# Convolution on one core: the overlap copied out once and added in PSUM to permuted block rows, one GELU per pass, group norm's sums on ScalarE

## Chip, cores and metric

The kernel runs on one core of one Trainium2 chip, as one program. The metric is device time in microseconds, the median of a few runs. TensorE (PE), VectorE (DVE), ScalarE (ACT) and GpSimd (POOL) are the engines; SP issues most of the loads.

## The reference

Two residual layers on `x` of shape 32 x 128 x 32 x 32 (32 images, 128 channels, L = 1,024 positions). Only the first layer matters here, and only up to the GELU:

```
u = group_norm(x)                         # 32 groups of 4 channels, per image
h = einsum('bdl,de->ble', u, W_enc) + b_enc        # 1,024 features
K = table of 64 taps per feature (from dt, A, C)
y = causal convolution of h with K along l, per feature
y = gelu_tanh(y + D * h)
...                                       # GLU, layer norm, decode, residual
...                                       # second layer: group norm, deformable convolution
```

## The kernel before, in words

The program has four parts in order. `ssm_kernel_table` works out the convolution's taps and writes them to `kp_d`. `normalise_input` runs group norm on each of the 32 images and stores the result in `u_d`. `ssm_convolution` reads `u_d` and writes the activated convolution to `y_d`. `main_block` does everything else: gated linear unit, layer norm, decode, and the second layer, in an order that is written out by hand. The first three parts are ordered by a scheduler, which lists the instructions of each engine from its own model of their times; every engine then works through its list in order.

`group_norm` (L161) takes one image of 128 partitions x 1,024. It sums the rows on VectorE (L164), averages over the four channels of a group with a matmul by `gavg` (L166), copies the mean (L168), subtracts it into `gn_cen` (L170), squares and sums on ScalarE (L173), averages again (L174), takes the root (L176) and the reciprocal (L177), and scales (L178). The pool has three buffers for each tile. The main block has a group norm of its own, in steps; `group_norm` is called apart from `normalise_input` only in a fallback branch.

`ssm_convolution` makes eight passes (`k`), each over 128 of the 1,024 features, and in each pass first encodes and then convolves.

- `encode(k)` goes over the 32 images and two halves of the sequence. Four matmuls (L227) fill a PSUM tile `psz` with 4 blocks of 128 positions x 128 features, and VectorE adds the bias and writes the tile into `z` (L234), with the image as the innermost index. After it, `z[0]` and `z[1]` hold for each feature a matrix of 128 positions by (4 blocks x 32 images).
- `convolve(k, z)` goes over 16 groups of `CG` = 8 features, each in two quarters (`q`) of `QC` = 4 features and two halves of the sequence (`i`). One such unit is one PSUM tile `psy` of two banks; three of them exist. Four matmuls (L266), one a feature, each multiply `z` by a Toeplitz table `toe` of 128 x 192: the 192 columns are the 128 outputs of a block and 64 outputs that reach over into the next block. The profile shows each of these matmuls as two records. The partitions of a unit are four blocks of 32 images, in the order of the sequence.

The 64 columns that reach over (`RW` = 64) must be added to the block that follows, which lies 32 partitions further. Before, a tile `t` in SBUF collects them: its first 32 rows are zeros written by GpSimd (`i` = 0, L275) or a copy from the end of the half before, out of that half's PSUM tile `last` (L277, VectorE); its other rows are three copies of 32 rows from PSUM (L280; the first on VectorE, the other two on ScalarE). VectorE then adds the unit's own columns (L284). ScalarE makes the GELU in two pieces, L286 from PSUM and L290 from `t`, and reverses the columns on the way. The result goes to `yo` (two tiles a group, four buffers), and GpSimd issues eight stores a group, one per tile and block (L296).

Of the kernel before, what the change touches and what calls it, by code (L numbers as in the profile page):

```python
# [7 lines left out]
F32 = mybir.dt.float32  # L8
AF = mybir.ActivationFunctionType
ALU = mybir.AluOpType  # L10
AX = mybir.AxisListType
# [3 lines left out]
P = 128  # L15
B, C, H, W = 32, 128, 32, 32
L = H * W
# [8 lines left out]
TW = 192  # L26
# [3 lines left out]
CG = 8  # L30
# [130 lines left out]
def group_norm(nc, pool, psum, gavg, eps, xt, out):  # L161

    s = pool.tile([P, 1], F32, tag="gn_s", name="gn_s")
    nc.vector.reduce_sum(s, xt, axis=AX.X)  # L164
    pm = psum.tile([P, 2], F32, tag="gn_ps", name="gn_ps")
    nc.tensor.matmul(pm[:, 0:1], gavg, s, start=True, stop=True)  # L166
    m = pool.tile([P, 1], F32, tag="gn_m", name="gn_m")
    nc.vector.tensor_copy(m, pm[:, 0:1])  # L168
    cen = pool.tile([P, L], F32, tag="gn_cen", name="gn_cen")
    nc.vector.tensor_scalar(cen, xt, m, None, op0=ALU.subtract)  # L170
    sq = pool.tile([P, L], F32, tag="gn_sq", name="gn_sq")
    ss = pool.tile([P, 1], F32, tag="gn_ss", name="gn_ss")
    nc.scalar.activation(sq, cen, AF.Square, accum_out=ss)  # L173
    nc.tensor.matmul(pm[:, 1:2], gavg, ss, start=True, stop=True)  # L174
    r = pool.tile([P, 1], F32, tag="gn_r", name="gn_r")
    nc.scalar.activation(r, pm[:, 1:2], AF.Sqrt, bias=eps)  # L176
    nc.vector.reciprocal(r, r)  # L177
    nc.vector.tensor_scalar(out, cen, r, None, op0=ALU.mult)  # L178


def normalise_input(nc, tc, const, x, u_d):

    with tc.tile_pool(name="gna", bufs=3) as pool, tc.tile_pool(
        name="gna_ps", bufs=2, space=PSUM
    ) as psum:
        for b in range(B):
            xt = pool.tile([P, L], F32, tag="xt", name=f"xt_{b}")
            nc.sync.dma_start(xt, x[b])
            u = pool.tile([P, L], F32, tag="u", name=f"u_{b}")
            group_norm(nc, pool, psum, const["gavg"], const["eps"], xt, u)  # L190
            nc.scalar.dma_start(u_d[b], u)


def ssm_convolution(nc, tc, ins, u_d, kp_d, y_d):

    NB = NJ // 2  # L200
    RW = TW - P
    QC = 4
    with tc.tile_pool(name="cv1", bufs=1) as one, tc.tile_pool(
        name="cvu", bufs=4
    ) as up, tc.tile_pool(name="cvt", bufs=3) as tp, tc.tile_pool(
        name="cvy", bufs=4
    ) as yp, tc.tile_pool(
        name="cv_psz", bufs=2, space=PSUM
    ) as psz, tc.tile_pool(name="cv_psy", bufs=3, space=PSUM) as psy:
        w_enc = one.tile([P, D], F32, tag="w_enc", name="w_enc")  # L210
        nc.sync.dma_start(w_enc, ins["W_enc"])
        b_enc = one.tile([P, D], F32, tag="b_enc", name="b_enc")
        nc.sync.dma_start(b_enc, ins["b_enc_row"].to_broadcast([P, D]))

        def encode(k):

            z = [
                one.tile([P, P, NB, B], F32, tag=f"z{g}", name=f"z_{k}_{g}") for g in range(2)
            ]
            bias = b_enc[:, k * P : (k + 1) * P]  # L220
            for b in range(B):
                u = up.tile([P, L], F32, tag="u", name=f"u_{k}_{b}")
                nc.sync.dma_start(u, u_d[b])
                for g in range(2):
                    ps = psz.tile([P, NB, P], F32, tag="ps", name=f"psz_{k}_{b}_{g}")
                    for j in range(NB):
                        nc.tensor.matmul(  # L227
                            ps[:, j, :],
                            u[:, (NB * g + j) * P : (NB * g + j + 1) * P],
                            w_enc[:, k * P : (k + 1) * P],  # L230
                            start=True,
                            stop=True,
                        )
                    nc.vector.tensor_add(  # L234
                        z[g][:, :, :, b].rearrange("p d j -> p j d"),
                        ps,
                        bias[:, None, :].to_broadcast([P, NB, P]),
                    )
            return z

        def convolve(k, z):
            rows = [t.rearrange("p d j b -> p d (j b)") for t in z]
            for g in range(P // CG):
                d0 = k * P + g * CG
                toe = tp.tile([P, CG, TW], F32, tag="toe", name=f"toe_{d0}")
                table = kp_d[d0 : d0 + CG, 0:TW]

                nc.sync.dma_start(
                    toe,
                    bass.AP(  # L250
                        tensor=table.tensor,
                        offset=table.offset,
                        ap=[[1, P], [KPW, CG], [1, TW]],
                    ),
                )
                yo = [
                    yp.tile([P, CG, P], F32, tag="yo", name=f"yo_{d0}_{i}") for i in range(2)
                ]
                for q in range(CG // QC):
                    c0 = q * QC  # L260
                    last = None
                    for i in range(2):
                        ps = psy.tile([P, 2, 512], F32, tag="ps", name=f"psy_{d0}_{q}_{i}")
                        ps = ps[:, :, : 2 * TW].rearrange("p h (c n) -> p h c n", c=2)
                        for c in range(QC):
                            nc.tensor.matmul(  # L266
                                ps[:, c // 2, c % 2, :],
                                rows[i][:, g * CG + c0 + c, :],
                                toe[:, c0 + c, :],
                                start=True,  # L270
                                stop=True,
                            )
                        t = tp.tile([P, 2, 2, RW], F32, tag=f"t{i}", name=f"t_{d0}_{q}_{i}")
                        if i == 0:
                            nc.gpsimd.memset(t[0:B], 0.0)  # L275
                        else:
                            nc.vector.tensor_copy(t[0:B], last[P - B : P, :, :, :RW])  # L277
                        for j in range(1, NB):
                            copy = nc.scalar.copy if j > 1 else nc.vector.tensor_copy
                            copy(  # L280
                                t[j * B : (j + 1) * B],
                                ps[(j - 1) * B : j * B, :, :, :RW],
                            )
                        nc.vector.tensor_add(t, t, ps[:, :, :, P:TW])  # L284
                        to = yo[i][:, c0 : c0 + QC, :].rearrange("p (h c) l -> p h c l", c=2)
                        nc.scalar.activation(  # L286
                            to[:, :, :, RW:P], ps[:, :, :, RW:P][:, :, :, ::-1],
                            AF.Gelu_apprx_tanh,
                        )
                        nc.scalar.activation(  # L290
                            to[:, :, :, 0:RW], t[:, :, :, ::-1], AF.Gelu_apprx_tanh
                        )
                        last = ps
                for i in range(2):
                    for j in range(NB):
                        nc.gpsimd.dma_start(  # L296
                            y_d[d0 : d0 + CG, :, i * NB + j, :].rearrange("d b l -> b d l"),
                            yo[i][j * B : (j + 1) * B],
                        )

        for k in range(KD):
            convolve(k, encode(k))


def deformable_general(nc, tc, const, ins, x1_d, out, image):
# [7 lines left out]
    with tc.tile_pool(name="gdf1", bufs=1) as one, tc.tile_pool(  # L313
# [27 lines left out]
        def prepare(b):  # L341

            xt = two.tile([P, L], F32, tag="xt", name=f"gen_dx_{b}")
            nc.sync.dma_start(xt, x1_d[bass.ds(image, 1)].rearrange("o c l -> (o c) l"))
            v = one.tile([P, L], F32, tag="v", name=f"gen_dv_{b}")
            group_norm(nc, one, psum, const["gavg"], const["eps"], xt, v)

            vT = two.tile([P, NCHUNK, C], F32, tag="vT", name=f"gen_dvT_{b}")
# [903 lines left out]
```

## Time and profile before

| | us |
|---|---|
| three runs: median (lowest, highest) | 14067.17 (14044.14, 14073.55) |
| profiled execution | 14059.14 |
| its span | 14057.0 |
| start to the first encode matmul (tables, group norm) | 178 |
| convolution, from there to the first instructions of the main block | 1,614 |
| main block | 12,265 |

Over the whole span TensorE is busy for 94%, VectorE for 63%, ScalarE for 23% and GpSimd for 65%. The shares differ by stage: in the convolution TensorE is busy for 1,370 of 1,614 us, with a granted clock of 0.95.

How to read the lines. A line of a timeline has the start, the busy time, the engine, the source line and operation, the tiles (written <- read), their shape and a count; in brackets the idle time before it and what ended that. A line of the chain of waits has start, length and what the chain went through. A group line has engine, operation, tiles, shapes and count, then the total busy time in us and the mean of one in ns, then the idle time before it in us by what ended it. A line of stages has the window, its length, and the busy time and count of PE, PE weight loads, DVE, ACT and POOL, then the granted TensorE clock, the share of the DMA engines and the rate.

### The profile page before, as it was taken

To read this page: it belongs to the slowest core of one execution; us is meant where nothing else is said; L and a number is where in the kernel's file an instruction comes from. 1 tells how busy PE (TensorE), PEld (TensorE's weight loads), DVE (VectorE), ACT (ScalarE), POOL (GpSimd) and SP (SyncE) were. 2 spreads that over 40 slices of the span, in tenths; PEclk is the share of its full clock that TensorE was granted. 3 is DMA by queue.
4 is the path that set the end of the run, shared out by engine and by line. 5 is a ranking of instruction groups with operands and counts; after the bars stand their busy time and mean duration, and the time that the engine had idled before them with its cause. 6 is when DMAs were issued, how large, how long until landed. Compare 5 with 4: busy or idle time off the path is not lost.

```text
span 14057.0 us, 134776 instructions
## 1 busy us (share of the span) xinstructions
PE 13268.5 (94%) x40482; PEld 7317.0 (52%) x40482; DVE 8827.7 (63%) x12555; ACT 3215.1 (23%) x5422; POOL 9113.7 (65%) x9158
## 2 busy tenths in 40 slices
PE   5888889999999999999999999999999999999965
PEld 4777744555555555555555555555555555555532
DVE  6666614666666666666666666666666666666655
ACT  3445412222222222222222121222222222222210
POOL 1334413777777777777777777777777777777767
PEclk9999999999999999999999999999999999999977
DMA  6777724888888888888888888888888888889888
GB/s 224 232 232 230 222 79 126 239 237 235 233 231 232 231 233 238 236 235 230 231 232 229 229 229 230 229 234 237 239 236 233 230 233 231 233 236 237 233 228 227
DMA packets 1741840, 3172.55 MB, mean 226 GB/s; under 512 B 311218, under 2 KB 1030450, under 8 KB 1740082
## 3 DMA queue, kind: packets, MB, share of 16 engines
q1 hardware_dynamic: 1528498, 2708.63, 72.9%
q10 hardware_dynamic: 163456, 320.92, 6.4%
q0 software_dynamic: 49152, 134.28, 3.1%
q8 instruction: 329, 5.39, 0.2%
q14 instruction: 405, 3.32, 0.1%
HBM read 2697.07 MB, written 466.06 MB: 225 GB/s over the span
## 4 chain that ended last, share of the span: by engine, by line
PE 75%; DMA 10%; DVE 7%; POOL 3%; issue 2%; ACT 2%; SPq 1%; DVEq 0%; ACTq 0%; POOLq 0%
PE gpg L707 22%; PE gpv L730 21%; PE dps L1032 21%; DMA ds<-dhat 6%; PE psz L227 4%; PE gph L746 3%; PE gpo L639 3%; DVE dco L839 2%; DVE ds L989 2%; POOL y_d L296 1%; DMA y_d<-yo 1%; PE psy L266 1%; DVE dp L1035 1%; ACT t L280 1%; DMA dhy<-dhat 1%
## 5 line engine op out<-in xcount | busy, mean ns | idle before, releaser
L1032 PE MATMUL dps<-ds,dxw 128*128 128x256 f32 (+18 forms) x13056 | 4737.7, 450 | 308.0 <-DVE dp L1035 305.7
L1035 DVE TENSOR_TENSOR dp<-dps,k_weight_slots 128x256 f32<-128x256 f32 (+17 forms) x6528 | 3061.5, 485 | 2868.8 <-PE dps L1032 2578.2
L1049 POOL TENSOR_TENSOR dacc<-dacc,dp 128x256 f32<-128x256 f32 (+3 forms) x4736 | 4224.6, 892 | 371.4
L1044 POOL TENSOR_TENSOR dp<-dp 128x512 f32<-128x512 f32 (+3 forms) x2176 | 2858.6, 1314 | 2159.3 <-DVE dp L1035 2140.9
L1032 PEld LDWEIGHTS dps<-ds,dxw 128*128 128x128 f32 x13056 | 2478.6, 193 | 3330.7 <-issue 2510.7
L707 PE MATMUL gpg<-gy,g_w_glu 128*128 128x512 f32 x8192 | 3986.6, 593 | 19.1 <-DMA gy<-y_d 14.3
L730 PE MATMUL gpv<-gy,g_w_glu 128*128 128x512 f32 x8192 | 3975.3, 592 | 0.0
L989 DVE TENSOR_TENSOR ds<-ds,dhy 128x1024 f32<-128x1024 f32 (+3 forms) x2176 | 3158.0, 1451 | 1242.4 <-DMA ds<-dhat 1165.3
L707 PEld LDWEIGHTS gpg<-gy,g_w_glu 128*128 128x128 f32 x8192 | 1544.6, 190 | 1235.2 <-issue 974.2
L730 PEld LDWEIGHTS gpv<-gy,g_w_glu 128*128 128x128 f32 x8192 | 1548.9, 189 | 1158.2 <-issue 915.2
L767 ACT ACTIVATE gq<-gr 128x512 f32<-128x512 f32 x448 | 282.3, 630 | 5050.9 <-DVE gr L759 4725.9
L768 POOL TENSOR_TENSOR gs<-gs,gq 128x512 f32<-128x512 f32 x448 | 599.1, 1337 | 1267.2 <-ACT gq L767 1267.1
L266 PE MATMUL psy<-toe,z 128*128 128x192 f32 x4096 | 790.2, 353 | 222.9 <-DVE t L277 214.8
L266 PEld LDWEIGHTS psy<-toe,z 128*128 128x128 f32 x4096 | 735.5, 207 | 273.4 <-issue 211.1
L714 ACT ACTIVATE gs<-gpg,k_b_glu 128x512 f32<-128x512 f32 x512 | 351.8, 687 | 2151.3 <-PE gpg L707 2078.9
L903 ACT ACTIVATE dh<-dr,k_minus 128x624 f32<-128x624 f32 x768 | 620.5, 808 | 933.4 <-DMA dr<-rel_d 493.5
L296 POOL DMA_DIRECT2D y_d<-yo x1024 | 589.1, 583 | 351.8 <-ACT yo L290 324.2
L738 DVE SCALAR_TENSOR_TENSOR gs<-gpv,k_b_glu,gs 128x512 f32<-128x512 f32 x512 | 379.9, 742 | 413.8 <-PE gpv L730 413.8
L641 POOL TENSOR_TENSOR gs<-gs,gr 128x512 f32<-128x512 f32 x448 | 635.3, 1418 | 0.0
L904 ACT ACTIVATE dh<-dh,one 128x624 f32<-128x624 f32 x768 | 626.3, 815 | 25.0
L227 PE MATMUL psz<-w_enc,u 128*128 128x128 f32 x4096 | 584.5, 288 | 24.0 <-DVE z L234 9.1
L275 POOL MEMSET t<- 32x256 f32 x256 | 72.4, 322 | 776.0 <-ACT yo L290 775.1
(164 smaller groups left out, 6620.3 us busy)
## 6 DMA issues: line engine op xcount, KB each, us to landing
dhy<-dhat SPq DMA_DIRECT2D x1536, 512.0 KB
ds<-dhat SPq DMA_DIRECT2D x1536, 512.0 KB
dhat<-dh ACTq DMA_DIRECT2D x768, 312.0 KB
u<-u_d SPq DMA_DIRECT2D x256, 512.0 KB
y_d<-yo POOLq DMA_DIRECT2D x1024, 128.0 KB, 3.7
gy<-y_d SPq DMA_DIRECT2D x512, 256.0 KB
toe<-kp_d SPq DMA_DIRECT2D x128, 768.0 KB
dxw<-dvt_d SPq DMA_DIRECT2D x1248, 64.0 KB
```

The lines of the kernel that those rows point to most:

```text
L227: nc.tensor.matmul(ps[:, j, :], u[:, (NB * g + j) * P : (NB * g + j + 1) * P], w_enc[:, k * P : (k + 1) * P], start=True, stop=True,)
L266: nc.tensor.matmul(ps[:, c // 2, c % 2, :], rows[i][:, g * CG + c0 + c, :], toe[:, c0 + c, :], start=True, stop=True,)
L296: nc.gpsimd.dma_start(y_d[d0 : d0 + CG, :, i * NB + j, :].rearrange("d b l -> b d l"), yo[i][j * B : (j + 1) * B],)
L641: nc.gpsimd.tensor_add(sums[0], sums[0], r)
L707: nc.tensor.matmul(gate, w_glu[:, k, D + m * P : D + m * P + P], ys[k], start=(k == 0), stop=(k == KD - 1),)
L730: nc.tensor.matmul(val, w_glu[:, k, m * P : m * P + P], ys[k], start=(k == 0), stop=(k == KD - 1),)
L904: nc.scalar.activation(t, t, AF.Relu, scale=-1.0, bias=const["one"])
L989: nc.vector.tensor_mul(s[:, :m], s[:, :m], hy[:, :m])
L1032: nc.tensor.matmul(ps, xw[:, j, :], s[:, :m, :, y0 : y0 + ny], start=True, stop=True)
L1035: nc.vector.tensor_mul(prod[:, :m, :, y0 : y0 + ny], ps, w[:, :, :, None].to_broadcast([P, m, KY2, ny]),)
L1044: nc.gpsimd.tensor_add(prod[:, :m, 0], prod[:, :m, 0], prod[:, :m, 1])
L1049: nc.gpsimd.tensor_add(to, to, prod[:, slot : slot + nj, 0])
```

## The change

In `group_norm`, both sums move to ScalarE: an Identity pass over the image with an accumulator, and a Square pass with the negated mean as bias, both writing into the output tile as scratch. The negated mean is made by ScalarE; the subtracted copy `gn_cen` and `gn_sq` are gone, and the last instruction adds the negated mean and scales in one.

In the convolution, the blocks of a half are laid on the partitions in the order 0, 2, 1, 3, by permuting the encode's columns and the stores' targets. The 64 columns that reach over are copied out of PSUM in one ScalarE copy of all 128 partitions. VectorE then adds them in place into the unit's own columns in PSUM: in this order blocks 0 and 2 (partitions 0 to 63) go to blocks 1 and 3 (partitions 64 to 127) in one add, block 1 goes to block 2 in a second, and the end of the half before goes to block 0 in a third (for `i` = 1 only). One GELU of 128 columns a feature follows. The memset and `last`'s hold on the PSUM tile are gone.

```diff
 def group_norm(nc, pool, psum, gavg, eps, xt, out):
     s = pool.tile([P, 1], F32, tag="gn_s", name="gn_s")
-    nc.vector.reduce_sum(s, xt, axis=AX.X)
+    nc.scalar.activation(out, xt, AF.Identity, accum_out=s)
...
-    nc.vector.tensor_copy(m, pm[:, 0:1])
-    cen = pool.tile([P, L], F32, tag="gn_cen", name="gn_cen")
-    nc.vector.tensor_scalar(cen, xt, m, None, op0=ALU.subtract)
-    sq = pool.tile([P, L], F32, tag="gn_sq", name="gn_sq")
+    nm = pool.tile([P, 1], F32, tag="gn_m", name="gn_m")
+    nc.scalar.mul(nm, pm[:, 0:1], -1.0)
     ss = pool.tile([P, 1], F32, tag="gn_ss", name="gn_ss")
-    nc.scalar.activation(sq, cen, AF.Square, accum_out=ss)
+    nc.scalar.activation(out, xt, AF.Square, bias=nm, accum_out=ss)
...
-    nc.vector.tensor_scalar(out, cen, r, None, op0=ALU.mult)
+    nc.vector.tensor_scalar(out, xt, nm, r, op0=ALU.add, op1=ALU.mult)
...
+    ORDER = (0, 2, 1, 3)
...
-                            u[:, (NB * g + j) * P : (NB * g + j + 1) * P],
+                            u[:, (NB * g + ORDER[j]) * P : (NB * g + ORDER[j] + 1) * P],
...
-                        t = tp.tile([P, 2, 2, RW], F32, tag=f"t{i}", name=f"t_{d0}_{q}_{i}")
-                        if i == 0:
-                            nc.gpsimd.memset(t[0:B], 0.0)
-                        else:
-                            nc.vector.tensor_copy(t[0:B], last[P - B : P, :, :, :RW])
-                        for j in range(1, NB):
-                            copy = nc.scalar.copy if j > 1 else nc.vector.tensor_copy
-                            copy(
-                                t[j * B : (j + 1) * B],
-                                ps[(j - 1) * B : j * B, :, :, :RW],
-                            )
-                        nc.vector.tensor_add(t, t, ps[:, :, :, P:TW])
-                        to = yo[i][:, c0 : c0 + QC, :].rearrange("p (h c) l -> p h c l", c=2)
+                        over = tp.tile([P, 2, 2, RW], F32, tag=f"t{i}", name=f"t_{d0}_{q}_{i}")
+                        nc.scalar.copy(over, ps[:, :, :, :RW])
+
+                        def carry(to, rows, src):
+                            own = ps[to : to + rows, :, :, P:TW]
+                            nc.vector.tensor_add(own, own, src)
+
+                        carry(64, 64, over[0:64])
+                        carry(32, 32, over[64:96])
+                        if i > 0:
+                            carry(0, 32, last[96:P])
                         nc.scalar.activation(
-                            to[:, :, :, RW:P], ps[:, :, :, RW:P][:, :, :, ::-1],
+                            yo[i][:, c0 : c0 + QC, :].rearrange("p (h c) l -> p h c l", c=2),
+                            ps[:, :, :, RW:TW][:, :, :, ::-1],
                             AF.Gelu_apprx_tanh,
                         )
-                        nc.scalar.activation(
-                            to[:, :, :, 0:RW], t[:, :, :, ::-1], AF.Gelu_apprx_tanh
-                        )
-                        last = ps
+                        last = over
...
-                            y_d[d0 : d0 + CG, :, i * NB + j, :].rearrange("d b l -> b d l"),
+                            y_d[d0 : d0 + CG, :, i * NB + ORDER[j], :].rearrange("d b l -> b d l"),
```

More of the change, by code (lines that the diff above doesn't have):

```diff
@@ L163, in group_norm @@
     s = pool.tile([P, 1], F32, tag="gn_s", name="gn_s")
-    nc.vector.reduce_sum(s, xt, axis=AX.X)
+    nc.scalar.activation(out, xt, AF.Identity, accum_out=s)
     pm = psum.tile([P, 2], F32, tag="gn_ps", name="gn_ps")
     nc.tensor.matmul(pm[:, 0:1], gavg, s, start=True, stop=True)
-    m = pool.tile([P, 1], F32, tag="gn_m", name="gn_m")
-    nc.vector.tensor_copy(m, pm[:, 0:1])
-    cen = pool.tile([P, L], F32, tag="gn_cen", name="gn_cen")
-    nc.vector.tensor_scalar(cen, xt, m, None, op0=ALU.subtract)
-    sq = pool.tile([P, L], F32, tag="gn_sq", name="gn_sq")
+    nm = pool.tile([P, 1], F32, tag="gn_m", name="gn_m")
+    nc.scalar.mul(nm, pm[:, 0:1], -1.0)
     ss = pool.tile([P, 1], F32, tag="gn_ss", name="gn_ss")
-    nc.scalar.activation(sq, cen, AF.Square, accum_out=ss)
+    nc.scalar.activation(out, xt, AF.Square, bias=nm, accum_out=ss)
     nc.tensor.matmul(pm[:, 1:2], gavg, ss, start=True, stop=True)
```

## The prediction

> **What bounds the kernel now.** I read the stages first, then the convolution stage's matmuls, its chain of waits and its operations. The stages (window, then busy microseconds by engine, clock, DMA share, GB/s):
>
> ```profile
> 0.00:178.00 178.00, 34.82 (x129) 31.11 (x129) 119.03 (x216) 56.37 (x109) 3.17 (x8) 1.00 0.65 228
> 178.00:1792.00 1614.00, 1369.70 (x8192) 1234.46 (x8192) 1063.00 (x1793) 710.96 (x2049) 660.41 (x1278) 0.95 0.76 227
> 1792.00:14057.00 12265.00, 11864.00 (x32162) 6051.47 (x32162) 7645.70 (x10546) 2447.76 (x3264) 8450.08 (x7873) 0.99 0.84 225
> ```
>
> The edit reaches 1,792 us of 14,057. The main block behind it has, in the built changed kernel, the same instructions in the same order. A convolution pass takes 201 us (first encode matmul at 177.97, last tile at 1788.5, eight passes): some 74 us encode, some 127 us convolve. A pass convolves 16 groups of 4 units; a unit is one PSUM tile, written by 8 matmul records. The timeline of TensorE in one pass:
>
> ```profile
> 875.17 7.12 PE L266 MATMUL psy<-toe,z 128*128 128x192 f32 x32 [2.85 <-DVE t L277]
> 882.74 5.81 PE L266 MATMUL psy<-toe,z 128*128 128x192 f32 x32 [0.45 <-DVE t L277]
> 891.89 7.12 PE L266 MATMUL psy<-toe,z 128*128 128x192 f32 x32 [3.34 <-DVE t L277]
> ...
> 941.73 5.44 PE L266 MATMUL psy<-toe,z 128*128 128x192 f32 x32 [3.34 <-DVE t L277]
> ```
>
> A line of 32 is one group. It goes in 5.44 us at best: 0.165 us a record, **1.31 us a unit** back to back, about 1.57 us from the start of a lone unit to its data. Every second group TensorE waits some 3.3 us, and then mostly runs its first records slowly (7.12 against 5.44). A pair takes 16.4 to 17.0 us: **8.22 us a group** (mean of the six pairs from 875.17 to 973.88). The chain of waits says why:
>
> ```profile
> 871.08 2.30 POOL y_d L296 x4
> 873.38 0.33 POOL t L275
> 873.71 0.02 issue
> 873.73 0.43 DVE t L284
> 874.16 0.02 issue
> 874.19 0.39 ACT yo L286
> 874.58 0.02 issue
> 874.60 0.44 DVE t L277
> 875.04 0.14 issue
> 875.17 2.87 PE psy L266 x8
> ```
>
> GpSimd zeroes the next pair's tiles only behind 16 stores; add, GELU and the copy of `last` wait for that, and so does the PSUM tile that TensorE needs.
>
> **What the skill says.** (1) "TensorE: Matmul & The Clock Gate", section "What's actually happening": the array drops to half clock after about 3.4 us of idleness and comes back after as long a busy stretch. The trace agrees in kind: pauses of 2.85 to 3.34 us are followed by slow records, though not always (941.73). (2) "PSUM — Partial Sum Buffer", "Engine vs sequencer instructions": ScalarE and VectorE are strict FIFO. In the windows read here their records keep the built order, so a built order may be read as a chain.
>
> **The change, part by part.** Durations of the convolution's operations, in the stage's groups:
>
> ```profile
> L280 ACT COPY t<-psy 32x256 f32<-32x256 f32 x1024 | 370.5, 362 | 696.9 <-DVE t L280 682.4
> L284 DVE TENSOR_TENSOR t<-t,psy 128x256 f32<-128x256 f32 x512 | 210.4, 420 | 268.8 <-ACT t L280 178.3 <-POOL t L275 87.1 <-ACT yo L286 0.7
> L286 ACT ACTIVATE yo<-psy 128x256 f32<-128x256 f32 x512 | 195.2, 381 | 211.6 <-DVE t L284 209.4
> ```
>
> *ScalarE.* Before, a unit has two copies and two GELUs (0.362 x 2 + 0.381 + 0.410 = 1.52 us). After, one copy of 128x256 (taken as 0.362, the partition count being no part of it) and one GELU of 128x512: 0.381 plus 256 elements at 0.833 ns (the skill's "ScalarE: Activation LUTs", "What ACT_TABLE_LOAD costs"; the trace has 1,055 ns for 1,024 and 630 for 512, or 0.830) = **0.594 us**. So 0.96 us a unit, 3.8 of some 8 us a group: this saving is off the path, but its duration is in the loop below.
>
> *VectorE.* Ten instructions a group before (4 L280, 2 L277, 4 L284), ten after: two adds per unit, three for the second half. Same count, no gain by itself. They write PSUM in place, which no record shows. Low end 0.42 (L284). The skill's "Perfetto Trace Analysis", "Optimizing Scalar/DVE Operations", gives 125 ns overhead on PSUM against 60 on SBUF: 0.49. High end 0.60: the encode add (1,045 ns for 512 elements with strided writes) less 0.15 fixed, scaled to 256. I take 0.45 start to start, as two of these instructions in a row take now.
>
> *GpSimd.* 256 memsets leave (72.4 us of its time), and with them the 3.3 us wait. Its stores stay: 8 x 0.583 = 4.66 us a group. A landing takes 3.7 us, and an output buffer is wanted again two groups later, some 12 us after its last GELU: covered up to landings of about 8.
>
> *What is late next.* In the built changed kernel ScalarE's list in 13 of 16 groups reads: GELU 0, GELU 2, copy 3, copy 0', GELU 1, GELU 3, copy 1', copy 2' (a prime is the next group). With three PSUM tiles, GELUs 0 and 2 free two, TensorE fills 3 and 0', and GELU 1, which frees the third, stands behind copy 0'. So half a loop is GELU 0.594 + release 0.06 + one unit issued 1.31 + the next one's data 1.57 + 0.03 + copy 0.362 + 0.02 = 3.95 us. **7.89 us a group**, with TensorE idle for 1.33 us twice. VectorE has room in it: with both copies of a pair 1.31 us apart and adds of d, GELU 2 ends 5d - 0.66 after the second copy, and TensorE is free for 0' at 1.96, so d may be 0.52.
>
> The sum for a pass:
> - 13 groups x (8.22 - 7.89) = -4.3 us.
> - The first three groups stand in another order (each GELU behind the copy two units on), which TensorE sets: 5.3 + 5.3 + 6.5 = 17.1 us. Before, 859.80 to 875.17 plus half of 16.7 = 23.7: -6.6.
> - The built order puts two encode tiles of the next pass ahead of the last unit. Each waits for a VectorE add (1.045 + 0.1) and takes TensorE 1.0 us; part of that is encode work done early: +3.5.
>
> That is -7.4 us a pass, **-59 us** for eight.
>
> *Permuted blocks* (the encode's column order, the stores' targets) keep count, size and shape of every matmul and DMA: nothing, whatever covers them.
>
> *Group norm.* VectorE loses a reduce (1.216), a subtract (0.744) and a copy an image; ScalarE gains an Identity pass and a small multiply. The stage now runs at 7.40 us per two images: the chain has the load of `xt` at 104.66 and again at 112.06, 4.55 us each, after the subtract that frees the buffer. After, `xt` is held to the last scale. In the built order, three images a round: Identity 1.06, store issue 0.34, mean back at 1.71, negate 0.15, Identity 1.06, Square 1.15, negate 0.15, Identity 1.06, Sqrt done at 5.5, VectorE's reciprocal and scale to 6.5, load 4.55: 11.1 us, 3.70 an image, as now. I put +5 us on it for ScalarE's queue, which now also holds the stores behind these passes (bounds -5 and +20). The copy of group norm in the fallback branch does not run: the trace has no record of it.
>
> Together -54 us. The profiled execution took 14,059 us (span 14,057), so 14,005; the median of the runs, 14,067, lies 8 us higher: **14,012 us**.
>
> **The rivals.**
> *Slower: the adds in PSUM are dear.* From d = 0.52 each further 0.01 us costs 0.05 us a group in 13 x 8 groups, 5.2 us, more once GELU 3 waits too. Break-even is near d = 0.61, and 0.66 gives +40 us: 14,110. For it: VectorE's adds stand between ScalarE's two instructions in every unit. Against: reading PSUM costs nothing visible now (0.420). Chance 0.09.
> *Slower: TensorE goes to half clock in its 1.33 us gaps.* One slow first unit a group costs 1.3 to 1.7 us (7.12 against 5.81 and 5.44): +140 us over 104 groups, 14,150. The end of the main block is the nearest case:
>
> ```profile
> 13604.91 3.57 PE L1032 MATMUL dps<-ds,dxw 128*128 128x288 f32 x6 [4.33 <-DVE dp L1035]
> 13609.67 3.57 PE L1032 MATMUL dps<-ds,dxw 128*128 128x352 f32 x6 [1.20 <-DVE dp L1035]
> 13614.40 1.97 PE L1032 MATMUL dps<-ds,dxw 128*128 128x416 f32 x6 [1.16 <-DVE dp L1035]
> 13618.40 2.34 PE L1032 MATMUL dps<-ds,dxw 128*128 128x480 f32 x6 [2.03 <-DVE dp L1035]
> ```
>
> Once quick, it stays quick over 1.16 and 2.03 us. Chance 0.06.
> *No change:* each of the loop's two halves being 0.2 us longer (GELU of reversed rows, copy) takes back 42 us, or landings slow beyond 8 us and GELUs wait for stores. 14,067, chance 0.17.
> *TensorE-bound throughout*, 5.3 us a group, as its idle time alone would promise: 2.6 x 104 = 270 us more, 13,740. ScalarE's order speaks against it. Chance 0.03.
>
> **How the numbers follow.** My forecast has 0.65, between 13,960 and 14,045 by the spread of the loop's terms (0.15 us in a half is 31 us) and of the first groups (3 us a pass). The range 13,935 to 14,105 takes in the no-change case and part of the dear adds, and leaves out the half clock and the TensorE-bound case. About 0.2%, 28 us, is what a measurement of this kernel can tell from no change. Faster by more: 0.67; within: 0.17; slower: 0.16.
>
> **What would show it.** Right: no wait on a memset; groups of matmuls split in pairs of units with gaps near 1.3 us, ended by GELU; in-place adds at 0.42 to 0.5; passes of some 194 us; the clock at 1.00 there. Wrong: adds above 0.6, slow matmuls after short gaps, idle time ended by stores, or normalisation longer than 150 us.

## The result, and the profile after

The changed kernel takes 14,004.9 us (median of four runs, 13,995.6 to 14,027.6), the kernel before 14,058.7 in four runs: a ratio of 0.9964, 95% interval 0.9947 to 0.9981. That is 54 us less. The forecast was 14,012 us and 55 us below the 14,067 known then.

The profiled execution of the changed kernel is the slowest of its four (14,027.6 us, span 14,025.8), so the two profiles differ by 31 us only. By the starts of TensorE's first records in each stage:

| us | before | after | difference |
|---|---|---|---|
| start to the first encode matmul | 178.0 | 200.7 | +22.8 |
| first encode matmul to the last of the convolution | 1,607.6 | 1,557.3 | -50.4 |
| from there to the main block's first matmul | 36.8 | 39.9 | +3.1 |
| main block | 12,234.6 | 12,227.9 | -6.7 |

The main block has the same instructions in the same order in both. The profiles of all fourteen kernels in this study, which share the main block, give 12,208 to 12,240 us for it, so the last row says nothing. The first two rows are far clearer than the medians.

The stages of the changed kernel (window, busy us by engine PE, weight loads, DVE, ACT, POOL, then clock, DMA share, GB/s):

```profile
0.00:178.00 178.00, 33.26 (x114) 28.48 (x114) 59.09 (x110) 87.93 (x183) 2.43 (x5) 1.00 0.57 202
178.00:1792.00 1614.00, 1305.43 (x8238) 1175.68 (x8238) 1083.93 (x1815) 470.80 (x1049) 590.15 (x1025) 0.98 0.77 236
```

In the first window VectorE's work has halved (119 to 59 us) and ScalarE's has grown (56 to 88), but the window moves fewer bytes: group norm has become slower. In the second the clock has risen from 0.95 to 0.98 and GpSimd has lost the 70 us of its zeros. (While passes are convolved the clock is 1.00, in 862:984 for instance; what is missing lies at the ends of passes, see below.)

TensorE's timeline in the pass that the prediction showed:

```profile
886.47 2.87 PE L266 MATMUL psy<-toe,z 128*128 128x192 f32 x16 [1.02 <-ACT yo L284]
890.36 2.87 PE L266 MATMUL psy<-toe,z 128*128 128x192 f32 x16 [1.02 <-ACT yo L284]
...
979.90 1.16 PE L227 MATMUL psz<-w_enc,u 128*128 128x128 f32 x8 [1.22 <-DVE z L234]
982.34 1.16 PE L227 MATMUL psz<-w_enc,u 128*128 128x128 f32 x8 [1.28 <-DVE z L234]
983.34 1.47 PE L266 MATMUL psy<-toe,z 128*128 128x192 f32 x8
```

The groups of 32 with a pause of 3.3 us in every second one are gone. There are pairs of units (16 records, 2.87 us) and 1.02 us of waiting for a GELU after each: 3.885 us from pair to pair (half of the loop of one group), **7.77 us a group**. No pair is slow. The last three lines are the end of the pass: two encode tiles ahead of the last unit, each after a wait for VectorE's add. The chain of waits of one half of the loop:

```profile
909.12 0.61 ACT yo L284
...
909.78 2.88 PE psy L266 x16
...
912.74 0.04 ACT t L274
...
913.01 0.61 ACT yo L284
...
913.66 1.58 PE psy L266 x8
```

A GELU frees a tile, TensorE fills two units, the copy of the second goes through ScalarE, and only behind it stands the next GELU that frees a tile. The convolution's operations (idle time before them behind the second bar):

```profile
L278 DVE TENSOR_TENSOR psy<-psy,t 32x256 f32<-32x256 f32 x768 | 327.3, 426 | 26.2
L284 ACT ACTIVATE yo<-psy 128x512 f32<-128x512 f32 x512 | 296.1, 602 | 103.7 <-DVE psy L278 101.8 <-DMA y_d<-yo 0.5
L278 DVE TENSOR_TENSOR psy<-psy,t 64x256 f32<-64x256 f32 x512 | 226.6, 443 | 364.8 <-ACT t L274 356.3
L274 ACT COPY t<-psy 128x256 f32<-128x256 f32 x512 | 190.5, 372 | 1004.7 <-PE psy L266 1004.7
```

The adds in PSUM cost 0.43 to 0.44 us, the GELU 0.602, the copy 0.372. ScalarE's GELUs wait for VectorE (101.8 us in all), not for stores (0.5); its copies wait for TensorE. The chain of waits in group norm:

```profile
144.47 6.62 DMA u_d<-u
...
151.11 1.15 ACT u L164 x2
152.26 0.15 ACT gn_r L173
152.40 1.12 ACT u L170 x2
153.52 4.72 DMA xt<-in_x
...
158.27 6.17 DMA u_d<-u
```

Here a store and a load alternate. The Identity pass of a round's third image writes into the output tile `u`, so it waits until the store of three images before has landed. The first image's root and scale stand behind it, then comes the load of the image that follows, and behind that image's Identity pass the next store is issued (158.27, though its data was ready at 157.8). A round of three images takes 12.3 to 13.8 us (the last seven rounds, 13.1 in the mean); before, three images took about 11.4 (the last twelve images).

### The profile page after: what moved, and what is told of

It reads as the page before. It is cut to its first block, busy times and chain, and to the rows that moved or that the text cites. A ratio compares the mean times of both kernels' runs of the same rounds, so it can differ in the third digit from the quotient of the medians.

```text
span 14025.8 us, 133165 instructions
## 1 busy us (share of the span) xinstructions
PE 13195.7 (94%) x40482; PEld 7248.1 (52%) x40482; DVE 8797.9 (63%) x12459; ACT 3004.9 (21%) x4494; POOL 9042.0 (64%) x8902
## 4 chain that ended last, share of the span: by engine, by line
PE 76%; DMA 10%; DVE 9%; issue 2%; POOL 1%; ACT 1%; SPq 1%; DVEq 0%; ACTq 0%; POOLq 0%
PE gpg L703 23%; PE gpv L726 21%; PE dps L1028 21%; DMA ds<-dhat 5%; PE gph L742 3%; PE gpo L635 3%; PE psy L266 2%; PE psz L227 2%; DMA y_d<-yo 2%; DVE z L234 2%; DVE dco L835 2%; DVE ds L985 2%; DVE dp L1031 1%; DVE psy L278 1%; DMA dhy<-dhat 1%
## 5 line engine op out<-in xcount | busy, mean ns | idle before, releaser
L266 PE MATMUL psy<-toe,z 128*128 128x192 f32 x4096 | 734.0, 333 | 203.3 <-ACT yo L284 203.1
L266 PEld LDWEIGHTS psy<-toe,z 128*128 128x128 f32 x4096 | 662.8, 191 | 268.8 <-ACT yo L284 266.8
L278 DVE TENSOR_TENSOR psy<-psy,t 32x256 f32<-32x256 f32 (+1 forms) x1280 | 553.9, 433 | 391.0 <-ACT t L274 356.3
```

The costliest lines, as they stand in the source:

```text
L266: nc.tensor.matmul(ps[:, c // 2, c % 2, :], rows[i][:, g * CG + c0 + c, :], toe[:, c0 + c, :], start=True, stop=True,)
L278: nc.vector.tensor_add(own, own, src)
```

## The experiments

Kernels whose convolution is ordered by hand begin to encode at 189 to 194 us instead of 175 with the same group norm, so the time of a pass compares them best. Their group norm, still left to the scheduler, takes 8.3 to 8.7 us for two images where conv_alone takes 7.3 (the last twelve images of each).

| kernel | median us | ratio to before (95%) | first encode | us a group |
|---|---|---|---|---|
| conv_alone | 13,988.9 | 0.9958 (0.9941 to 0.9974) | 174.9 | 7.77 |
| norm_scratch | 14,007.1 | 0.9963 (0.9949 to 0.9977) | 191.3 | 7.77 |
| norm_bufs | 13,980.6 | 0.9941 (0.9924 to 0.9957) | 161.3 | 7.77 |
| hand_built | 14,043.4 | 0.9989 (0.9982 to 0.9996) | 193.2 | 7.77 |
| gelu_split | 14,058.5 | 0.9997 (0.9988 to 1.0006) | 193.4 | 7.89 |
| adds_more | 14,042.9 | 0.9988 (0.9980 to 0.9997) | 175.1 | 8.08 |
| hand_unit | 13,862.0 | 0.9862 (0.9844 to 0.9879) | 189.4 | 6.3 |
| hand_unit_yo6 | 13,797.0 | 0.9812 (0.9796 to 0.9828) | 193.6 | 5.8 |
| memset_dve | 14,363.2 | 1.0211 (1.0193 to 1.0228) | 174.6 | 11.5 |
| hand_before | 14,088.4 | 1.0018 (1.0010 to 1.0025) | 190.4 | 8.1 |
| hand_before_early | 13,995.8 | 0.9961 (0.9946 to 0.9975) | 189.2 | 7.3 |
| best | 13,756.1 | 0.9783 (0.9767 to 0.9799) | 156.8 | 5.8 |

(In hand_unit, hand_unit_yo6, hand_before, hand_before_early and best, us a group is the time of convolving a pass, first matmul of it to the next pass's first encode, over 16.)

**conv_alone: the convolution's part alone.** The edit puts the old `group_norm` back.

```diff
-    nc.scalar.activation(out, xt, AF.Identity, accum_out=s)
+    nc.vector.reduce_sum(s, xt, axis=AX.X)
...
```

> The changed convolution with the group norm of before. In the changed kernel the first encode matmul starts at 200.7 us (before: 178.0) and the convolution takes 1,557 us (before: 1,608). If the two parts are independent, the first encode starts at 178 (176 to 181) and the convolution keeps 1,557 (1,550 to 1,565): some 23 us faster than the changed kernel, about 13,982 against a 14,005 and 0.9945 of before. Rival: the late start is partly given back in the convolution (loads that had more time), then the convolution takes 1,570 to 1,580 here and the gain over the changed kernel is under 10 us.

The first encode starts at 174.9 us, just ahead of the 176 expected, and the convolution takes 1,556.0 us against 1,557.3. The parts are independent: what group norm loses is not given back later. The whole gain is the convolution's, and the median is 16 us below the changed kernel's, where 23 were expected.

**norm_scratch: a scratch tile for the two passes of group norm.**

```diff
+    sq = pool.tile([P, L], F32, tag="gn_sq", name="gn_sq")
-    nc.scalar.activation(out, xt, AF.Identity, accum_out=s)
+    nc.scalar.activation(sq, xt, AF.Identity, accum_out=s)
```

> The changed kernel, with a scratch tile of its own for the outputs of the Identity and the Square pass in group norm, instead of the output tile. Theory: a round of three images takes 13.4 us because the Identity pass of the third image waits for the store of the output tile of three images before (6.2 us from issue to landing), and with it on ScalarE's queue the Sqrt of the first image, its scale and then the load of the next image (5.0 us), behind whose Identity the next store stands: 6.2 + 2.4 + 5.0. Without the hold on the output tile the round falls to about 11.1 us and the first encode starts at 178 (175 to 184); no Identity waits for a store. Rival: ScalarE's longer list and the later release of the input tile set the round by themselves: the first encode stays at 196 to 201.

The first encode starts at 191.3 us, between the two expectations. No Identity pass waits for a store any more, and a round falls from 13.1 to 11.9 us, not to 11.1. So the hold of the store on `u` is 9 of the 23 us. The rest hangs on the load: in the chain of this kernel it takes 6.7 us from an image's Identity pass to its scale and the issue of the load that this releases, and 5.06 for the load.

**norm_bufs: six buffers in group norm's pool instead of three.**

```diff
-    with tc.tile_pool(name="gna", bufs=3) as pool, tc.tile_pool(
+    with tc.tile_pool(name="gna", bufs=6) as pool, tc.tile_pool(
```

> The changed kernel with six instead of three buffers for group norm's tiles. With a scratch tile of its own a round of three images fell from 13.4 to 11.9 us only; what was left went over a load: the Sqrt of the first image stands behind the Identity pass of the third, and the input tile is free only after the scale behind it (7.1 us after the image's start, then 4.8 us of load). Theory: with six buffers neither the load nor the store is waited for, and ScalarE's own work of about 3.2 us an image sets the pace: the first encode starts at 160 to 172 us, before the 178 of before. Rival: the waits between ScalarE and TensorE inside an image (0.68 us each) or the DMA rate hold it at 3.7 us or more an image: 178 or later.

The first encode starts at 161.3 us, 39 us earlier than in the changed kernel and 17 earlier than before. ScalarE's waits in the stage (us in all, times, longest) show why, first in the changed kernel, then here:

```profile
ACT u L164 <- DMA xt<-in_x: 26.3, 20, 5.2
ACT u L164 <- DMA u_d<-u: 10.6, 8, 3.2
```

```profile
ACT u L164 <- DMA xt<-in_x: 1.1, 2, 0.7
```

No row for stores is left. ScalarE now works through two images in about 6.0 us. So with six buffers the changed group norm costs nothing against before. Whether it is a gain by itself is not shown: no run gives the old group norm six buffers. In the profile of before VectorE is busy for 86 us between 40 and 175 us, 2.7 us an image by that figure, so the old one might come near the 3.0 us an image seen here (an estimate).

**adds_more: one in-place add more in every unit of the sequence's first half.**

```diff
-                        if i > 0:
-                            carry(0, 32, last[96:P])
+                        carry(0, 32, last[96:P] if i > 0 else none)
...
```

`none` is a tile of zeros, written once.

> The changed convolution with the group norm of before, and one add more in every first half: 32 rows of zeros added in place in PSUM (0.43 to 0.46 us of VectorE each, 256 in all; the sums stay the same). In the trace of the changed kernel GELU 2 waits 0.56 us for the second of two units' adds and its end leaves 0.14 us until TensorE would want the tile. Theory: the first 0.14 us of the new add are free, the other 0.32 us lengthen one half of the loop: 7.77 becomes 8.1 us a group, 13,989 becomes some 14,025. Rival 1: VectorE is off the path (busy 0.56 of the convolving stretch): no change, 7.77. Rival 2: both halves take the whole add: 8.7 us a group, 14,100.

TensorE's timeline:

```profile
522.06 3.19 PE L272 MATMUL psy<-toe,z 128*128 128x192 f32 x16 [1.02 <-ACT yo L289]
526.26 2.87 PE L272 MATMUL psy<-toe,z 128*128 128x192 f32 x16 [1.02 <-ACT yo L289]
```

One half of the loop stays at 3.89 us, the other becomes 4.20: TensorE's 16 records stretch to 3.19 us because the second unit waits for its tile. A group takes 8.08 us against 8.1 expected; the convolution takes 32 us longer (1,588.2 against 1,556.0). Both rivals are out: VectorE is neither free nor wholly on the path. Of each 0.46 us, 0.14 is free.

**hand_built and gelu_split: the control, and the GELU in two pieces.** hand_built emits the changed convolution in a fixed order (shortened):

```diff
+            for n in range(0, N, 4):
+                gelu(n)
+                gelu(n + 2)
+                for m in (n + 3, n + 4): ...   # matmuls, copy, adds
+                gelu(n + 1)
+                gelu(n + 3)
+                for m in (n + 5, n + 6): ...
```

> Control for the next kernel: group norm of before, the changed convolution with every engine's order written out by hand, ScalarE in the order that the built changed kernel has in 13 of 16 groups: GELU 0, GELU 2, copy 3, copy 0', GELU 1, GELU 3, copy 1', copy 2'. Expected: the same 7.77 us a group in all 16 groups, pauses of 1.02 us ended by GELU; a pass within 5 us of 194.8 us (no encode tile ahead of the last unit: -3.5; the first groups in the slow order: +5.5). About 14,000 us. If writing the order out changes something else (loads of the tables later, say), idle time ended by a DMA shows it.

The group is 7.77 us from the second group on (7.94 once a pass) and a pass 197.4 us, as expected. The median is 43 us above the expected one: the passes account for 21 us, and the first encode is 18 us late, which I had not foreseen. gelu_split cuts the GELU into two of 64 columns a feature:

> The hand-written order of the changed kernel (7.77 us a group), with each GELU cut into two of 64 columns a feature, as before the change, one behind the other. In the kernel before two such GELUs take 0.70 us from the start of the first to the end of the second, the one GELU takes 0.60. Theory: the GELU stands in both halves of the loop: 0.1 us more in each, 0.2 us a group, 26 us over 128 groups: 8.0 us a group, 14,069 against the control's 14,043. Rival: ScalarE has room (busy for half of the time) and the cut costs nothing; or the second piece's start adds its whole 0.28 us: 8.3 us a group, 70 us more.

The pause is 1.08 us instead of 1.02, a group takes 7.89 us, and a pass is 1.9 us longer. The pair of pieces takes 0.67 us, not 0.70, so the price is 0.06 us a half instead of 0.10. The GELU does stand in both halves of the loop. In this order, joining the two pieces is worth about 15 us.

**hand_unit and hand_unit_yo6: another order on ScalarE.**

```diff
+            for n in range(N + 1):
+                if n < N:
+                    matmuls(n)
+                    copy(n)
+                    adds(n)
+                if n:
+                    gelu(n - 1)
```

> As the control, but ScalarE goes unit by unit: copy n, GELU n-1, copy n+1, GELU n. Theory: the 7.77 us a group come from the order alone (the GELU that frees the third PSUM tile stands behind the copy of a unit that TensorE can only begin after another GELU). Then a GELU ends 1.0 us after the next unit's last matmul, before TensorE has finished the unit behind it (1.31 us), and TensorE no longer waits for PSUM: 5.3 us a group if nothing else comes, but the DMA engines are busy for 0.79 of 7.77 us a group now, 6.1 us, and stores (8 x 0.58 us to issue, 4 us to land, buffers for two groups) may come next: 6.1 to 6.7 us a group, 100 to 170 us less than the control over 128 groups, some 13,850. Rival 1: VectorE's adds or ScalarE's sum of work set the pace, then the group stays at 7.5 to 7.8 and the time at the control's. Rival 2: nothing else comes, 5.3 us a group, 300 us less.

A pass falls from 197.4 to 176 us on average, with the same instructions and the same buffers: the order alone held the changed kernel at 7.77 us a group. What comes next is in ScalarE's waits while a pass is convolved:

```profile
ACT yo L307 <- DMA y_d<-yo: 13.0, 11, 3.8
ACT yo L307 <- DVE psy L297: 0.4, 2, 0.2
```

GELUs wait for output tiles whose stores have not landed. With six buffers instead of four (`name="cvy", bufs=6`):

> The unit-by-unit order with six instead of four output buffers `yo`. In the unit-by-unit kernel a group takes 6.26 us and ScalarE's idle time is ended by stores of `yo` (13.0 us of a pass of 100 us). Theory: with buffers for three groups that wait goes, and TensorE is next with 5.47 us a group, or the DMA engines (0.86 busy now): 5.5 to 5.9 us a group, 45 to 95 us less than 13,862. Rival: the DMA engines set 6.26 us already, and the stores are only where it shows: no change within 15 us.

The row for stores falls to 4.4 us, the group to 5.8 us, the time by 65 us. Two thirds of the groups take 5.41 us, with TensorE busy throughout, and the DMA engines are busy for 0.93 of the time while a pass is convolved (435:526): neither has much left.

**memset_dve: the zeros of before written by VectorE.**

```diff
-                            nc.gpsimd.memset(t[0:B], 0.0)
+                            nc.vector.memset(t[0:B], 0.0)
```

> The kernel before, with the zeros written by VectorE instead of GpSimd; nothing else. Theory: in before, the 3.3 us in which TensorE waits in every pair of groups are GpSimd's zeros standing behind 16 stores. Then these waits go, and with them the slow matmuls after them: the pair falls from 16.4 to between 13 and 15.5 us (VectorE gains 4 instructions a pair, and another wait of ScalarE's list comes next), 60 to 130 us for all passes, 13,930 to 14,000 - as much as the changed convolution brings or more. Rival: the zeros only end last in a wait that the PSUM tiles held by the copy of the half before would impose anyway; then the pair stays above 15.9 us and the time within 30 us of before.

It is 301 us slower, and neither theory is tested: the scheduler built another order for every engine from this one line. TensorE's timeline:

```profile
532.21 2.87 PE L266 MATMUL psy<-toe,z 128*128 128x192 f32 x16 [1.68 <-ACT yo L286]
537.36 2.84 PE L266 MATMUL psy<-toe,z 128*128 128x192 f32 x16 [2.28 <-DVE t L277]
542.25 4.55 PE L266 MATMUL psy<-toe,z 128*128 128x192 f32 x16 [2.05 <-ACT yo L286]
```

TensorE now waits after every two units, and part of the pairs run slowly. The question needed the old order kept fixed.

**hand_before and hand_before_early: the zeros' place on GpSimd, and nothing else.** hand_before writes out the order of before; hand_before_early moves only the zeros. The edit in words:

```diff
 # GpSimd, groups 2p and 2p+1
-zeros for both groups, stores of both groups
+zeros for the next group, stores of this group
```

> Control for the next kernel: the convolution of before with every engine's order written out by hand, as the built kernel before has it in one of its passes (GpSimd: four tiles' zeros, then sixteen stores). Expected: 16.4 to 17.0 us a pair of groups with TensorE waits of 2.8 to 3.3 us as in before, 126 to 130 us to convolve a pass, and a time within 30 us of before (the first encode starts some 15 us later, as in the other hand-ordered kernels).

> The same, with one difference in GpSimd's order: the zeros for group n+1 stand ahead of the stores of group n, not behind the stores of two groups. Moving them to VectorE had made the scheduler build another order for all engines (11.5 us a group), so that said nothing on the wait. Theory: GpSimd's zeros are the whole of the 3.3 us wait in a pair; without it VectorE's and ScalarE's chain per unit (copy, two copies, add, GELU, copy of `last`) sets 6.6 to 7.3 us a group, 105 to 117 us to convolve a pass against 128 in the control: 85 to 180 us less for eight passes, more than the change itself gained. Rival: behind the zeros another wait of nearly the same length ends (the PSUM tile that the copy of `last` holds): then 120 us or more a pass, less than 65 us gained.

The control convolves a pass in 129.3 us (mean of eight), the other in 116.7: 101 us less for eight passes, 93 in the medians. The first line is a pair's wait in the control, the second in the other:

```profile
524.26 5.44 PE L318 MATMUL psy<-toe,z 128*128 128x192 f32 x32 [3.35 <-DVE t L328]
```

```profile
533.91 5.44 PE L318 MATMUL psy<-toe,z 128*128 128x192 f32 x32 [2.33 <-DVE t L328]
```

The size of the gain is as the theory has it, the reason only half: the wait shrinks from 3.35 to 2.33 us instead of going, because the copy of `last` on VectorE still ends late. Idle time before the convolution's matmuls falls by some 6.4 us a pass, half of the 12.6. The rest comes from slow matmuls, more than half of which go with it (62 records a pass in the control, 26 in the other, 0.32 us from start to start where the quick ones have 0.16; 7.12 us for 32 records becomes 5.44 where all are quick).

**best: unit by unit, six output buffers, the changed group norm with six buffers.**

> Unit-by-unit order with six output buffers (13,797 us), and the changed group norm with six buffers instead of the one of before. In the scheduler-ordered kernels these put the first encode at 161 instead of 175 us. If the parts add up, the first encode starts 10 to 20 us earlier than the 193.6 of the kernel without, some 13,782. Rival: where the convolution's order is written by hand, the loads of its weights wait for the end of group norm's stores, and part of the gain is lost: within 5 us of 13,797.

The first encode starts at 156.8 us, 37 earlier than without the new group norm and its buffers, where 10 to 20 were expected, and the kernel takes 13,756 us: 306 us below before, 249 below the changed kernel. Some of the 37 is the slower group norm of the hand-ordered kernels (8.7 us for two images in hand_unit_yo6), which is 6.0 here as in norm_bufs.

## Why the prediction was right, and where it was not

*The loop.* It was forecast at 3.95 us a half and measured at 3.885, with the parts where the working put them. (The 1.33 us of idle time show as 1.02, because the profile counts a pair as busy up to its last record's end, 2.87 us instead of 2 x 1.31.) hand_built shows the loop by itself, hand_unit that ScalarE's order is its cause, gelu_split that the GELU is one of its terms.

*The adds in PSUM.* 0.45 us was taken, about 0.46 start to start is measured (five in 2.30 us). The 65 ns more that the prediction took for its 0.49 from the Trainium skill, "Perfetto Trace Analysis", section "Optimizing Scalar/DVE Operations", do not show: 0.426 and 0.443 us against 0.420 for an add that reads PSUM and writes SBUF. The 0.52 us up to which the adds were to cost nothing was a little generous: with 0.14 us free over five adds it lies at 0.49. That rival was closer than it was made to look.

*Gaps and clock.* No pair after a pause of 1.02 us is slow; the rival of half clock fell for the loop. It came true in a small place that the prediction did not look at, the two encode tiles ahead of the last unit: in five of seven passes the second of them is slow, and the unit behind it (1.16 and 1.47 us where they are quick, as in the pass shown above).

```profile
397.02 2.08 PE L227 MATMUL psz<-w_enc,u 128*128 128x128 f32 x8 [1.28 <-DVE z L234]
```

*The zeros.* "With them the 3.3 us wait" was too simple. The wait did go, since the whole chain behind it went. But as hand_before_early shows, only 1.0 of the 3.3 us was the zeros' doing, and another place on their queue gained more against its control (93 us in the medians) than the change did.

*The first groups and the encode tiles.* The first three groups take about 17.4 us (17.1 forecast). From the end of the unit before it to the end of the last unit is 7.4 us on average, slow records included; hand_built, without the tiles, takes 2.6. The way from there to the next convolution is 1.5 shorter than before (71.1 for 72.6 us): +3.3, where 3.5 was put down. The sum came out, but its reason did not hold whole: some of the price is slow matmuls.

*The sum for the convolution was mis-sized on the side of before.* -59 was forecast, the profiles have -50 (passes two to seven: 200.6 to 194.6, or -48 for eight). The changed side was right to 1 us a pass. But 13 x 8.22 + 23.7 = 130.6 us was taken for the old side, from one pass's first groups and six pairs. The stage itself gives 128.3 (mean of eight, from the first matmul of a convolution to the next encode). These 2.3 us a pass, 18 in all, were never there to be gained. The 23.7 counts from 859.80, where that pass's convolution has already run for five microseconds, and adds half a pair:

```profile
854.75 4.14 PE L266 MATMUL psy<-toe,z 128*128 128x192 f32 x24
```

The first three groups take 22.9 us in the mean of all passes, so the slip cost 0.8. The other thirteen take 105.1 up to the end of the last unit and not 106.9, since the last one ends without the pause that is in the mean of 8.22. (The range of 16.4 to 17.0 us a pair also leaves out one of the six pairs, 941.73 to 957.13, with 15.4.) The check was at hand: the prediction's own first paragraph has some 127.

*Group norm is the step that failed.* +5 was forecast (-5 to +20), +22.8 came (+26 against the 174.9 of conv_alone, which has the old group norm too). The forecast round of 11.1 us charged the load of `xt`, but left out that `u`, now scratch from the first pass on, is held by its store. It also took 4.55 us for a load that takes 4.7 to 4.9 here (5.0 to 5.3 in norm_scratch), and 6.5 us for a way that takes about 6.7. norm_scratch prices the store at 9 us, norm_bufs shows that with buffers enough the whole loss goes.

*The permuted blocks* were put down at nothing. No run tests them by themselves. The stores take a little longer to land (4.3 us for 3.7, medians), and the GELUs wait 0.5 us in all for them.

*The total* agrees better than its parts. In the profiles the two errors leave 31 us where 54 were forecast. The medians differ by 54, and one median is good to 10 to 15 us; this agreement is partly luck. That the kernel became faster, and that it came from the convolution, is not.

## What to carry to other kernels

Read a built order as a loop: find which instruction frees the buffer that the slowest engine wants, and what stands in front of it in its queue; here one exchange on ScalarE was worth three times the change. When a tile is written earlier than before (an output used as scratch), its store's landing enters the loop, and so does everything behind the waiting instruction. Sum the old side of a forecast against the stage's own time before subtracting.

## What the runs showed of the hardware that was not expected

- Slow matmuls come after shorter pauses than the 3.4 us of the Trainium skill, "TensorE: Matmul & The Clock Gate", section "What's actually happening": in memset_dve after 2.05 to 2.28 us, where the busy stretches between are 2.8 to 4.6 us, and at the ends of the changed kernel's passes after pauses of 1.22 and 1.28 us with 1.16 us of work between them. After pauses of 1.02 us with stretches of 2.87 there are none. In these runs the length of a pause alone does not tell.
- An add of 32 rows costs about as much as one of 64 or 128 (0.426, 0.443 and 0.420 us for 256 columns), though the first two write to PSUM and the third to SBUF.
